# An attention-and-experts kernel: the remainders of the experts in blocks of two halves, and the last stage with rows added three pieces later

## The chip, the cores and the metric

The kernel runs on one NeuronCore of a Trainium2 chip. The core has five engines that run side by side, each through its own list of instructions in order: TensorE (matrix products, in the profile PE, its weight loads PEld), VectorE (DVE), ScalarE (ACT), GpSimd (POOL) and SyncE (SP), which here does nothing but issue transfers. Sixteen DMA engines carry the transfers between main memory (HBM) and the on-chip memory (SBUF). The metric is the device time of one execution in microseconds (us); lower is better.

## The reference

The reference normalises each row of `x` (4 batches of 1024 rows, 512 wide) and adds two things to the row: causal attention with 16 heads of width 32 and a distance penalty (ALiBi), and a mixture of experts.

```python
xn = _layernorm(x, axis=-1)
x = x + _L0_attn_ref(xn, Wq, bq, ..., Wo, bo) + _L0_ffn_ref(xn, gate_w, w1, w2)

# _L0_ffn_ref: 8 experts, each row goes to its best two
logits = jnp.einsum('th,eh->te', x, gate_w)
topw, sel = jax.lax.top_k(_softmax(logits), 2)
topw = topw / jnp.sum(topw, axis=-1, keepdims=True)
gate_up = jnp.einsum('th,eoh->eto', x, w1)      # 512 -> 2 * 352
g, u = jnp.split(gate_up, 2, axis=-1)
expert_out = jnp.einsum('eti,ehi->eth', _silu(g) * u, w2)   # 352 -> 512
out = jnp.einsum('eth,te->th', expert_out, combine)
```

The kernel computes an expert only for the rows that chose it: 4096 rows with two choices are 8192 (row, expert) pairs. All values are float32.

## The kernel before

**Routing.** After the layer norm (rows kept in HBM as `xr_d`, their transposes as `xn_d`), `route` (lines 479 to 594) sorts the pairs by expert on DVE: it counts the pairs of each expert, rounds the count up to whole blocks of 128, and gives each pair a slot (`slot`), each block an expert (`eid`) and each slot a row (`token`). With 8 experts whose counts are not known at build time, rounding up can take 71 blocks (`NBLK`, line 76), so 71 blocks are always computed, whatever share of them is padding. A few projections stand between the pieces of `route` on PE.

**Experts.** `expert_pieces` (lines 675 to 805) makes three pieces a block. `gate(k)` transposes the activation of block k-1 (`pact`) and multiplies the block's rows by the first half of the expert's `w1` (`pgate`: four products of 128 x 352); `up(k)` multiplies by the second half (`pup`), issues the loads of the next block's `w1` (four transfers of 352 KB from SP, line 684) and transposes the next block's rows (`pxs`); `second_layer(k)` multiplies block k-1 by `w2` (`ye`: three products of 512 columns), stores the result in `ys_d` (line 786), issues the next `w2` loads (line 695), and has POOL gather the rows of block k+3. Tiles of `w1` come from a ring of six buffers, those of `w2` from a ring of four. A load waits, on SP, until the last reader of its buffer is done, and everything behind it on SP waits with it.

**Attention.** Sixteen units (4 batches x 4 groups of 4 heads) of 12 groups g each. For a group, PE makes scores (`s`), the products that find each row's maximum for the next unit (`m`), and probabilities times values (`o`); ACT takes exponentials, DVE maxima and sums. The `o` products use 128 x 32 pieces of the array: the four heads are four products side by side in four strips of 32 columns.

**The last stage.** `final_pieces` (lines 812 to 862) finishes rows in 32 pieces of 128: `load(i)` issues from SP the rows of `x` (`xr`, line 819) and, for batches 0 to 2, the attention output (`ot`, line 824), and from POOL two gathers of expert rows (`g`, line 828), one for each choice. `piece(i)` adds the two gathered tiles to `xr` on DVE (line 850), multiplies `ot` by `Wo` on PE (`y`, line 840), adds the product to `xr` on DVE (line 843) and stores `xr` from SP (line 844). Every fourth piece belongs to batch 3, whose attention is still being computed: it has no `ot` and no product here, and its rows are held until `rest`. `final_all` (lines 1117 to 1139) puts the pieces in order and loads three pieces ahead: `load` of piece k+3, then `piece(k)`. `xr` and `ot` have four buffers each, `g` eight.

**Order.** The order on every engine is the order of the program. `fill` (lines 1187 to 1213) spreads the list `fills` (expert pieces, then pieces of the last stage, each with a weight) over the groups of the attention, so that at every group the weights spent keep pace with an even rate. A piece of the experts or of the last stage thus stands in PE's list between attention products, and an engine whose next instruction waits does nothing else meanwhile.

Of the kernel before, what the change touches and what calls it, by code (L numbers as in the profile page):

```python
# [16 lines left out]
P = 128  # L17
# [11 lines left out]
def kernel(  # L29
# [46 lines left out]
    NBLK = (T * TOP - NE) // BLK + NE  # L76
# [6 lines left out]
    eid = const.tile([P, NBLK], U32, tag="eid", name="eid")  # L83
# [29 lines left out]
    with ExitStack() as actx:  # L113
# [287 lines left out]
        def set_route():  # L401
# [13 lines left out]
            steps = ramp("steps", NB, BLK)  # L415
# [63 lines left out]
        def route():  # L479

            def prefix(src, n, name):
# [8 lines left out]

            more = after_norm("more", [P, NE, NB])
# [4 lines left out]
                ALU.is_gt,  # L496
            )
            blocks = once("blocks", [P, NE])
            nc.vector.tensor_reduce(blocks, more, mybir.AxisListType.X, ALU.add)
            ends = prefix(blocks, NE, "ends")  # L500
            first = once("first", [P, NE])
            nc.vector.tensor_tensor(first, ends, blocks, ALU.subtract)
            nc.vector.tensor_scalar(first, first, float(BLK), None, ALU.mult)
            rank = once("rank", [P, NT, NE])
            nc.vector.tensor_tensor(
                rank, p_rank, first.unsqueeze(1).to_broadcast([P, NT, NE]), ALU.add
            )
            slotf = once("slotf", [P, TOP, NT])
            for j in range(TOP):
# [3 lines left out]

            bnum = once("bnum", [P, NBLK])
            over = after_norm("over", [P, NBLK, NE])
            nc.vector.tensor_tensor(
                over,
                iota_row[:, :NBLK].unsqueeze(2).to_broadcast([P, NBLK, NE]),
                ends.unsqueeze(1).to_broadcast([P, NBLK, NE]),
# [3 lines left out]
            nc.vector.tensor_scalar(eid, bnum, float(NE - 1), None, ALU.min)  # L523
# [150 lines left out]

        def expert_pieces():
            es, w1s, w2s, rows, xsT, acts, actT = {}, {}, {}, {}, {}, {}, {}

            def load_w1(k):
                if k == NBLK:
                    return  # L680
                es[k] = nc.sync.value_load(eid[0:1, k : k + 1], min_val=0, max_val=NE - 1)
                for c in range(NC):
                    w = phase["ex"].tile([P, 2, FI], F32, tag="w1", name=f"w1_{k}_{c}", bufs=6)
                    nc.sync.dma_start(
                        w.rearrange("p g f -> p (g f)"),
                        w1r[bass.ds(es[k], 1), :, c, :].rearrange("o p f -> p (o f)"),
                    )
                    w1s[k, c] = w

            def load_w2(k):  # L690
                if k == NBLK:
                    return
                for f, (f0, m) in enumerate(FCH):
                    w = phase["ex"].tile([P, E], F32, tag="w2", name=f"w2_{k}_{f}", bufs=4)
                    nc.sync.dma_start(
                        w[:m, :],
                        w2T[bass.ds(es[k], 1), f0 : f0 + m, :].rearrange("o p e -> p (o e)"),
# [3 lines left out]
            def load_rows(k):  # L701
                if k >= NBLK:
                    return
# [9 lines left out]
            def turn(k):  # L713

                if k == NBLK:
# [7 lines left out]

            def half_up(k, gu):

                ps = bank([P, FI], F32, name=f"p{('gate', 'up')[gu]}_{k}")
                for c in range(NC):
                    nc.tensor.matmul(  # L728
# [8 lines left out]
            def gate(k):  # L737
                turn_act(k - 1)
                if k == NBLK:
                    return  # L740
                ps = half_up(k, 0)

# [5 lines left out]
            def up(k):  # L748
# [4 lines left out]
                load_w1(k + 1)  # L753
                turn(k + 1)

            def turn_act(k):
                if k < 0:
# [12 lines left out]
            def down(k):  # L770
                if k < 0:
                    return
                y = bank([P, E], F32, name=f"ye_{k}")
                a = actT.pop(k)
                for f, (_, m) in enumerate(FCH):
                    nc.tensor.matmul(  # L776
                        y,
                        lhsT=a[:m, f, :],
                        rhs=w2s.pop((k, f))[:m, :],
                        start=(f == 0),  # L780
# [585 lines left out]
```

## Time and profile before

| what | value |
|---|---|
| time, median of 3 runs | 1636.28 us (1635.67 to 1639.81) |
| the profiled execution's own time | 1648.37 us |
| its span, first to last instruction | 1646.6 us |
| PE busy | 1612.0 us, 98% |
| DVE, ACT, POOL busy | 939.4, 890.0, 332.5 us |
| moved by DMA | 278.94 MB, 169 GB/s on average |
| granted TensorE clock, mean | 0.997 of full |

Busy is time in which an instruction of the engine ran; an engine's waiting shows as an idle time in front of an instruction, with what ended it. A product of float32 operands is two MATMUL records on PE, so `pgate ... x568` is 71 blocks x 4 products x 2. SP's rows (SPq) are the issues of transfers, not the transfers themselves. All windows and starts are in us from the span's start.

### The profile page before, as it was taken

Reading aid. Unit: us, or ns where it says so; the run is one execution under the profiler, and the core shown is the slowest. Engines: PE = TensorE matmul, PEld = TensorE weight load, DVE = VectorE, ACT = ScalarE, POOL = GpSimd, SP = SyncE. Lnnn points to the kernel's source line nnn. Section 1 sums busy time; section 2 is a strip of 40 time slices with the busy share of each in tenths; the row PEclk is TensorE's granted clock in tenths of the full one; section 3 lists DMA queues with packets and bytes.
Section 4 is the critical chain, followed back from the end, with each engine's and each line's share of the span. In section 5 each row is a group of like instructions: output and inputs, shape, how many; then the busy total and the mean of one; then the engine's idle time right before and its main releaser. Section 6 shows DMA issues by size and latency. Waiting matters only on the chain.

```text
span 1646.6 us, 29019 instructions
## 1 busy us (share of the span) xinstructions
PE 1612.0 (98%) x9476; PEld 785.9 (48%) x9476; DVE 939.4 (57%) x2886; ACT 890.0 (54%) x2062; POOL 332.5 (20%) x762
## 2 busy tenths in 40 slices
PE   7999999999999999999999999999999999979999
PEld 4545545545454544545544445454444445433333
DVE  6775555655646555555555555555555555547652
ACT  5443455565656465656556474646565565646331
POOL 4610011111020102021111112010211011133660
PEclk9999999999999999999999999999999999999999
DMA  9847854547542434456452335464533424356891
GB/s 312 334 138 255 276 168 155 193 132 237 168 135 89 144 125 146 145 184 209 136 161 88 116 97 174 147 232 153 171 124 105 137 90 156 119 188 200 275 300 64
DMA packets 146486, 278.94 MB, mean 169 GB/s; under 512 B 16448, under 2 KB 45120, under 8 KB 144800
## 3 DMA queue, kind: packets, MB, share of 16 engines
q1 hardware_dynamic: 134384, 234.89, 43.3%
q0 software_dynamic: 10800, 35.40, 7.4%
q10 hardware_dynamic: 1152, 6.82, 1.0%
q8 instruction: 75, 1.23, 0.3%
q14 instruction: 75, 0.61, 0.1%
HBM read 229.07 MB, written 47.97 MB: 168 GB/s over the span
## 4 chain that ended last, share of the span: by engine, by line
PE 88%; DMA 2%; issue 1%; ACT 1%; DVE 1%; SPq 0%; another core or an unknown queue 0%; DVEq 0%; ACTq 0%
PE ye L776 11%; PE pup L728 11%; PE pgate L728 10%; PE s L1007 10%; PE o L1084 8%; PE m L893 8%; PE pk L622 6%; PE pq L622 6%; PE y L840 6%; PE pv L654 5%; PE s L1026 2%; PE pxs L721 2%; PE pact L762 2%; DMA w<-in_w1T 2%; DMA ot<-o_d 1%
## 5 line engine op out<-in xcount | busy, mean ns | idle before, releaser
L1038 ACT ACTIVATE pr<-s,kbias 128x512 f32<-128x512 f32 (+3 forms) x768 | 382.6, 581 | 387.9 <-PE s L1026 345.9
L939 ACT ACTIVATE z<-z,top 128x896 f32<-128x896 f32 (+7 forms) x512 | 391.5, 773 | 84.0 <-DVE top L929 81.0
L1046 POOL TENSOR_SCALAR_AFFINE_SELECT pr<-pr 128x128 f32<-128x128 f32 x512 | 150.4, 302 | 1105.5 <-ACT pr L1038 1099.0
L917 DVE CUSTOM_DVE_ANT_0 z<-m,rel 128x512 f32<-128x512 f32 (+3 forms) x512 | 271.5, 586 | 101.5 <-PE m L893 101.0
L776 PE MATMUL ye<-w,actT 128*128 128x512 f32 (+1 forms) x426 | 197.9, 600 | 2.1 <-DVE actT L765 2.1
L728 PE MATMUL pgate<-w,xsT 128*128 128x352 f32 x568 | 183.9, 464 | 1.8 <-DMA w<-in_w1T 1.4
L728 PE MATMUL pup<-w,xsT 128*128 128x352 f32 x568 | 182.4, 464 | 0.2 <-ACT pr L1038 0.2
L1007 PE MATMUL s<-q,k 32*128 32x512 f32 (+3 forms) x1536 | 179.4, 533 | 0.0
L893 PE MATMUL m<-k,q 32*128 32x512 f32 (+3 forms) x1536 | 172.5, 487 | 4.9 <-DVE oT L1099 4.8
L917 DVE CUSTOM_DVE_ANT_0 z<-m,rel,l 128x128 f32<-128x128 f32 (+3 forms) x256 | 125.8, 547 | 86.6 <-PE m L893 86.1
L1084 PE MATMUL o<-pr,v 128*32 128x512 f32 (+3 forms) x1536 | 144.9, 492 | 0.0
L728 PEld LDWEIGHTS pup<-w,xsT 128*128 128x128 f32 x568 | 105.6, 190 | 68.7 <-ACT pr L1038 9.9
L728 PEld LDWEIGHTS pgate<-w,xsT 128*128 128x128 f32 x568 | 101.5, 190 | 54.3 <-DMA w<-in_w1T 6.2
L622 PE MATMUL pq<-xnT,wq 128*128 128x512 f32 x256 | 119.6, 610 | 1.3 <-ACT pr L1038 0.8
L776 PEld LDWEIGHTS ye<-w,actT 128*128 128x128 f32 (+1 forms) x426 | 76.6, 190 | 90.7 <-issue 72.5
L622 PE MATMUL pk<-xnT,wk 128*128 128x512 f32 x256 | 117.8, 603 | 0.7 <-ACT pr L1038 0.7
L654 PE MATMUL pv<-wv_sb,xnT 128*128 128x512 f32 x256 | 117.0, 600 | 0.2 <-ACT pr L1038 0.2
L1007 PEld LDWEIGHTS s<-q,k 32*128 32x128 f32 x1536 | 61.1, 183 | 108.9 <-issue 82.3
L893 PEld LDWEIGHTS m<-k,q 32*128 32x128 f32 x1536 | 87.2, 185 | 45.5 <-issue 11.7
L745 DVE SCALAR_TENSOR_TENSOR th<-th,pgate 128x352 f32<-128x352 f32 x71 | 37.0, 521 | 121.7 <-ACT th L744 121.7
L939 ACT ACTIVATION_READ_ACCUMULATOR z<-z,top 128x1 f32 x512 | 100.4, 196 | 0.0
L840 PE MATMUL y<-wo_sb,ot 128*128 128x512 f32 x192 | 90.8, 622 | 6.0 <-DMA ot<-o_d 6.0
(165 smaller groups left out, 1564.1 us busy)
## 6 DMA issues: line engine op xcount, KB each, us to landing
w<-in_w1T SPq DMA_DIRECT2D x284, 352.0 KB
w<-in_w2T SPq DMA_DIRECT2D x142, 256.0 KB
ys_d<-yr SPq DMA_DIRECT2D x71, 256.0 KB
w<-in_w2T SPq DMA_DIRECT2D x71, 192.0 KB
xr<-in_x SPq DMA_DIRECT2D x32, 256.0 KB
out<-xr SPq DMA_DIRECT2D x32, 256.0 KB
xn_d<-xT ACTq DMA_DIRECT2D x6, 1024.0 KB
o_d<-oT SPq DMA_DIRECT2D x24, 256.0 KB
```

Source lines behind the costliest of these rows:

```text
L622: nc.tensor.matmul(ps, lhsT=ws[which][:, i, :], rhs=xnT[b, s][:, i, :], start=(i == 0), stop=(i == NC - 1),)
L654: nc.tensor.matmul(ps, lhsT=xnT[b, t // QT][:, i, (t % QT) * P : (t % QT + 1) * P], rhs=wv_sb[:, i, :], start=(i == 0), stop=(i == NC - 1),)
L728: nc.tensor.matmul(ps, lhsT=xsT[k][:, c, :], rhs=w1s[k, c][:, gu, :], start=(c == 0), stop=(c == NC - 1),)
L776: nc.tensor.matmul(y, lhsT=a[:m, f, :], rhs=w2s.pop((k, f))[:m, :], start=(f == 0), stop=(f == NF - 1),)
L840: nc.tensor.matmul(y, lhsT=lhsTs[c], rhs=wo_sb[:, c, :], start=(c == 0), stop=(c == NC - 1))
L893: nc.tensor.matmul(pss[h][:, col : col + n], lhsT=qs[b, c, s][r, (i % QT) * P : (i % QT + 1) * P], rhs=ks[b, c, k0 // QB][r, :n], start=Tr ...
L917: nc.vector.tensor_tensor_reduce(out=zs[h][:, z0 : z0 + n], in0=pss[h][:, col : col + n], in1=rel[:, S - L + k0 : S - L + k0 + n], scale=1 ...
L939: nc.scalar.activation(z[h][:, z0 : z0 + L], z[h][:, z0 : z0 + L], AF.Exp, bias=top[:, h : h + 1], scale=-slopes[c * HC + h], accum_out=to ...
L1007: nc.tensor.matmul(ps[:, :n], lhsT=ks[b, c, j // QT][r, (j % QT) * P : (j % QT + 1) * P], rhs=qs[b, c, s][r, q0:], start=True, stop=False,)
L1038: nc.scalar.activation(pr[:, :n], pss[h][:, :n], AF.Exp, bias=kbias[:, hh, d : d + 1], scale=-slopes[hh],)
L1046: nc.gpsimd.affine_select(out=pr[:, :P], in_=pr[:, :P], compare_op=ALU.is_ge, fill=0.0, base=0, pattern=[[1, P]], channel_multiplier=-1,)
L1084: nc.tensor.matmul(o[h * D : (h + 1) * D, q1:], lhsT=vs[b, j][:, col : col + D], rhs=prs[h][:, : QB - q1], start=(k == 0), stop=(k == len( ...
```

## The change

Three things change together.

**Blocks of two halves.** Only full blocks of an expert stay blocks of one expert: 57 of them (`PURE`, 8192/128 - 7). What is left of each expert (less than 128 pairs) is rounded up to halves of 64, and two halves, of one or of two experts, make a mixed block: 11 of them, in all 68 blocks. A mixed block is spread evenly among the others in the order `blocks`. Its products are made in strips: four products with 32 of the block's columns each, two with the weights of the first half's expert and two with those of the second (`strips`), in `gate`, `up` and `down`. It so needs the weights of two experts: eight `w1` transfers of 352 KB (six at once, the last two after `gate`) and eight for `w2` in two parts of half the columns, out of the same rings of six and four buffers. Where a mixed block is concerned, `down` of the block before moves ahead of `up`, and its own `down` is two parts, one on each side of the next `up`. `route` computes the layout by halves on DVE, with some 27 instructions more.

**First rows of the last stage.** `x` rows and attention output of the first three pieces go into buffers that are left over by then (one of `xnT`, and that of `Wv`); their loads are issued four pieces before the end of the experts, and the first product `y` stands before the last `down`.

**Gathered rows later.** `piece(i)` is now the product `y` and its addition alone. A new `join(i)` adds the two gathered tiles, and then stores; it stands in the step of piece i+3 (sooner at the end). Loads are issued in the step two pieces ahead, after that step's `join`, in place of three pieces ahead; gathers follow the join. The rings keep their sizes (`xr` and `ot` four, `g` eight).

```diff
-    NBLK = (T * TOP - NE) // BLK + NE
+    HALF = BLK // 2
+    PURE = T * TOP // BLK - (NE - 1)
+    NBLK = PURE + (2 * (NE - 1) + NE) // 2
...
+            full = small("full")
+            nc.vector.tensor_reduce(full, more, mybir.AxisListType.X, ALU.add)
...
+            nc.vector.tensor_tensor(rank, p_rank, every_tile(rows_full), ALU.is_ge)
+            nc.vector.tensor_tensor(rank, rank, every_tile(far), ALU.mult)
+            nc.vector.tensor_tensor(rank, rank, every_tile(first), ALU.add)
+            nc.vector.tensor_tensor(rank, rank, p_rank, ALU.add)
...
+            for n in range(NBLK - PURE):
+                blocks.insert((n + 1) * NBLK // (NBLK - PURE) - 3, PURE + n)
...
+                if mixed(k):
+                    load_two(k, 0, 0)
+                    load_two(k, 0, 2)
+                    load_two(k, 1, 0)
+                    return
...
+            def load_two(k, gu, c):
+                for i, e in enumerate(es[k]):
+                    w = w1_tile(f"{k}_{gu}_{c}_{i}")
+                    nc.sync.dma_start(
+                        w,
+                        w1r[bass.ds(e, 1), :, c : c + 2, gu * FI : (gu + 1) * FI].rearrange(
+                            "o p c f -> p (o c) f"
+                        ),
+                    )
...
+            def strips(ps, tokens, ws, **flags):
+                for q in range(P // D):
+                    cols = slice(q * D, (q + 1) * D)
+                    nc.tensor.matmul(
+                        ps[cols, :],
+                        lhsT=tokens[:, cols],
+                        rhs=ws[q * D // HALF],
+                        skip_group_check=True,
+                        **flags,
+                    )
...
             def gate(k):
...
                 ps = half_up(k, 0)
+                if mixed(k):
+                    load_two(k, 1, 2)
...
+                elif mixed(j):
+                    downs = [(1.5, lambda j=j, part=part: down(j, part)) for part in range(2)]
+                else:
+                    downs = [(2.8, lambda j=j: down(j))]
+                if mixed(k) or j is not None and mixed(j):
+                    pieces += downs[:1] + ups + downs[1:]
+                else:
+                    pieces += ups + downs
...
             def piece(i):
+                xr, o = held[i][:2]
+                if o is not None:
+                    project(b * ST + i, xr, [o[:, c, :] for c in range(NC)])
+
+            def join(i):
                 t = b * ST + i
-                xr, o, gs = held[i]
+                xr, o, *gs = held[i]
                 for j in range(TOP):
                     nc.vector.scalar_tensor_tensor(
                         xr, gs[j], share[:, t, j : j + 1], xr, ALU.mult, ALU.add
                     )
                 if o is not None:
-                    project(t, xr, [o[:, c, :] for c in range(NC)])
+                    store(t, xr)
...
             def prime():
-                for ops_, i in order[:ahead]:
-                    ops_[0](i)
+                o = qkv.tile([P, NC, QB], F32, tag="xnT", name="ot_first", bufs=2)
+                xr = wp.tile([P, NC, E], F32, tag="wv", name="xr_first")
+                for n, (op, i) in enumerate(order[:ahead]):
+                    op[0](i, xr[:, n, :], o[:, :, n * P : (n + 1) * P])
...
+            def late(k):
+                back = (len(order) - 1 - k) // 2
+                return min(back, 3)
...
-                def one(k=k, ops_=ops_, i=i):
-                    if k + ahead < len(order):
-                        nxt, ni = order[k + ahead]
+                def one(k=k, op=op, i=i):
+                    join(k - max(late(k), 1))
+                    if ahead <= k + ahead - 1 < len(order):
+                        nxt, ni = order[k + ahead - 1]
                         nxt[0](ni)
-                    ops_[1](i)
+                    gathered(min(k + 2, unjoined[0] + 3))
+                    if k > 0:
+                        op[2](i)
+                    join(k - late(k))
...
-        PROJ, JOIN = 3.6, 1.5
-        fills = [(0.0, begin_experts)] + expert_pieces() + [(0.0, begin_final), (3.0, finals[0])]
-        fills += [(JOIN if k % B == B - 1 else PROJ, f) for k, f in enumerate(finals[1:])]
+        PROJ, JOIN = 3.6, 0.6
+        fills = [(0.0, begin_experts)] + expert_pieces()
+        fills.insert(len(fills) - 4, (0.0, finals[0]))
+        fills.insert(len(fills) - 1, (PROJ, finals[1]))
+        fills += [(0.0, begin_final), (0.0, finals[2]), (0.0, finals[3])]
+        fills += [(JOIN if k % B == B - 2 else PROJ, f) for k, f in enumerate(finals[4:])]
```

## The prediction

> **What bounds the kernel now.** I read the busy times and the chain first, then the windows by stage, then PE's waits in the last stage.
>
> ```profile
> PE 1612.0 (98%) x9476; PEld 785.9 (48%) x9476; DVE 939.4 (57%) x2886; ACT 890.0 (54%) x2062; POOL 332.5 (20%) x762
> PE 88%; DMA 2%; issue 1%; ACT 1%; DVE 1%; SPq 0%; another core or an unknown queue 0%; DVEq 0%; ACTq 0%
> ```
>
> PE is the bound: only work taken off PE, or waits of PE, move the time. The windows tell where it waits (columns: stretch, its length, PE busy, PEld, DVE, ACT, POOL, granted clock, DMA share, GB/s).
>
> ```profile
> 80.00:106.00 26.00, 22.95 (x106) 11.66 (x105) 23.57 (x35) 12.35 (x26) 1.42 (x2) 1.00 0.03 6
> 160.00:1450.00 1290.00, 1286.21 (x7893) 631.04 (x7893) 718.46 (x2253) 749.63 (x1755) 187.77 (x513) 1.00 0.47 152
> 1450.00:1490.00 40.00, 30.77 (x165) 12.91 (x164) 19.71 (x55) 16.03 (x42) 17.46 (x27) 0.91 0.63 204
> 1490.00:1600.00 110.00, 105.59 (x555) 43.71 (x558) 76.46 (x161) 47.43 (x100) 65.37 (x82) 0.98 0.84 267
> ```
>
> In the expert stage PE idles 3.8 of 1290 us. In the routing (80 to 106) DVE is the busy one. The last stage has the rest, with DMA at 0.84. PE's waits from 1450 on:
>
> ```profile
> PE y L840 <- DMA ot<-o_d: 6.0, 4, 2.4
> PE m L893 <- DVE oT L1099: 4.8, 2, 4.0
> PE ye L776 <- DVE actT L765: 2.1, 1, 2.1
> PE pi L1063 <- DVE l L917: 0.6, 1, 0.6
> ```
>
> Together 13.5 us. Two of these waits are followed by slow products; a `y` of eight records takes 3.6 to 3.7 us otherwise:
>
> ```profile
> 1484.26 5.87 PE L840 MATMUL y<-wo_sb,ot 128*128 128x512 f32 x8
> ...
> 1552.09 5.37 PE L840 MATMUL y<-wo_sb,ot 128*128 128x512 f32 x8 [2.37 <-DMA ot<-o_d]
> ```
>
> **Part 1, three blocks fewer.** A block on PE, start to start in the timeline:
>
> ```profile
> 733.36 2.63 PE L728 MATMUL pup<-w,xsT 128*128 128x352 f32 x8
> 735.83 0.60 PE L721 MATMUL pxs<-ident,xs 128*128 128x128 f32 x4
> 736.27 2.74 PE L776 MATMUL ye<-w,actT 128*128 128x512 f32 x6
> 738.94 0.93 PE L1007 MATMUL s<-q,k 32*128 32x384 f32 x8
> ...
> 748.39 0.55 PE L762 MATMUL pact<-ident,act 128*128 128x128 f32 x3
> 748.78 2.53 PE L728 MATMUL pgate<-w,xsT 128*128 128x352 f32 x8
> 751.14 2.53 PE L728 MATMUL pup<-w,xsT 128*128 128x352 f32 x8
> ```
>
> `pup` 2.47, `pxs` 0.44, `ye` 2.67, `pact` 0.39, `pgate` 2.36: 8.33 us. Three blocks: **-25.0 us**. Their DVE and ACT work lies beside PE and gains nothing.
>
> **Part 2, eleven blocks in strips.** No row of before has these; the nearest are the `o` products, four strips of 128*32 side by side. In the chain a run of two strip sets takes 1.85 us (512+512 columns), 1.64 (512+384) or 0.79 (256+128): 1.64 ns a column and 0.17 us a run. A `gate` or `up` is then 4 x 352 x 1.64 ns + 0.17 = 2.48 us (2.36 to 2.47 now), a `down` 2 x (3 x 256 x 1.64 ns + 0.17) = 2.86 (2.67 now): 0.1 + 0.1 + 0.2 = 0.4 a block, **+4.5 us**; from -4, if a long run of strips hides its start (four runs of 0.17 a block less), to 8. The Trainium skill (TensorEngine Tiling (Array Packing), Tiling Modes, Key Properties) speaks against it: changing the tiling mode drains the array, with no price given. Taken as additional, another 0.17 for each of the 44 runs would make 7.5 more, 12 in all; but the `o` runs already change modes on both sides, so the 0.17 holds the drain, and I keep the row.
>
> **Part 3, weights of two experts.** SP issues 9 loads more for each mixed block; at some 0.55 us each that is beside PE. Six of eight `w1` tiles start at once. The tight place is the block after: no `down` stands between the mixed `up` and the next `gate`, and in PE's order six of the eleven gaps are 0.9 to 1.9 us. The last two `w1` tiles of that block wait for the second product of the mixed `up`, 1.2 us before its end; a 352 KB load lands 3.1 (quiet) to 4.2 us (median) after issue, from the trace's semaphores, so at 2.0 to 3.5 after the end of `up`. They are read 1.2 and 1.9 us into `gate`: up to 1 us late, six times. In two of the blocks the loads stand behind the `w2` loads of a `down` just before: 2 us more each. Rows are shorter (1408 and 1024 bytes in place of 2816 and 2048); packets of 512, 2048 and 2816 bytes take 27, 84 and 112 ns, so a mixed block costs 11.7 us of all 16 engines against 5.4, in a cycle of 20. I take **+4 us**, from 0 to 55 (5 a block, if every load is late by that difference).
>
> **Part 4, routing.** DVE runs without a break from 78.6 to 102.6 and PE waits for it at 97.40:
>
> ```profile
> 81.07 0.42 DVE L505 TENSOR_TENSOR rank<-routing,first 128x256 f32<-128x256 f32 x1
> 97.40 1.19 PE L539 MATMUL routing<-both,place 128*128 128x142 bf16 x16 [2.16 <-DVE both L572]
> ```
>
> New: 13 small instructions and a prefix sum of 6 at 0.16 (3.1), three `rank` steps at 0.43 (1.3), a table of 352 elements made and reduced at 0.53 each with three small steps (1.6), less 0.3 for a smaller `over`: 5.7 us, all before the first `place`. PE has no work to cover it: **+5.5 us** (3 to 7).
>
> **Part 5, the last stage.** The waits at its beginning go: `y` of the first three pieces has its rows early, and joins no longer stand in front of it: -13.5, and -5.1 for the slow clock after two waits (below).
>
> What is late next: a buffer of `xr` is now held from its load, two steps before the product, to the store after the join, three steps behind. With four buffers and three of four pieces using them, the load for a product waits for the landing of the store that SP issued just before it. In SP's order it stands directly behind that store, with that store's semaphore. Before, one other store lay between. Queued behind the load on SP: its `ot` load, the next store, the next loads. PE waits for `ot`. At `y8` (counting products from 0) the chain to `y10` is: addition of `y8` 0.85 after its end, two joins at 0.75, issue of the store 0.4, its landing, issue of `xr` 0.5, then `ot`. Landing of a store: 2.05 (the 71 `ys_d` stores, median) to 3.6, the store of 1544.73 here, which released the load of 1548.35:
>
> ```profile
> 1544.73 0.34 SPq L844 DMA_DIRECT2D out<-xr  x1
> ...
> 1546.06 0.52 SPq L824 DMA_DIRECT2D ot<-o_d  x1
> 1546.98 0.34 SPq L844 DMA_DIRECT2D out<-xr  x1
> 1548.35 0.33 SPq L819 DMA_DIRECT2D xr<-in_x  x1
> ```
>
> I take 2.6. Landing of `ot`: 3.7 (the same 256 KB in 512-byte pieces as `wq`, quiet) to 5.9 (the `ot` of 1546.06, for which PE waited at 1552.09); I take 4.5. Sum 10.4 us; 9.0 to 12.6. Beside it lie, in PE's order, only `y9` (3.5) and a group's narrow scores (1.1): 4.6. So `y10` waits **5.8 us** (4.4 to 8). The same place recurs every three products: before `y7` (where the join stands behind four maxima on DVE), `y10`, `y13`, `y16`, `y19`: 5 x 5.8 = 29. Before `y4`, whose load follows the first join, 4; before `y21` 1.5. In all **+34** (25 to 50). The gathers, issued three to four steps ahead of the join, are covered by 15 us and cost nothing; without that cover each join, and so each of these loads, would be late by what is missing.
>
> **The clock.** Windows 1470 to 1490 and 1540 to 1560 were granted 0.83 and 0.91 of the clock: half speed for 6.8 and 3.6 us, after waits of 4.0 and 2.4 us, so 3.4 and 1.8 us lost. The Trainium skill (TensorE: Matmul & The Clock Gate, Part 1) has the array throttle to half after an idle window of about 3.4 us and recover after 3.4 us of work, which is 1.7 lost a time: five waits make 8.5; by the rows' mean of 2.6, **+12.5**. A wait of 2.4 us sufficed here, which is shorter than the page's window; I take the rows.
>
> **Sum.** -25.0 + 4.5 + 4 + 5.5 - 18.6 + 34 + 12.5 = **+17 us**. The profiled execution took 1648.4 us around its span of 1646.6, 12 above the median of the timed runs; the difference is applied to the median: **1653 us**.
>
> **Rivals.**
> 1. Late loads in the last stage, as summed: 1653, with its own ends (parts 2 to 5) 1640 to 1672. Chance 0.55.
> 2. The loads come in time: if store and `ot` land so quickly, or joins run so early, that the 10.4 us fit in the 4.6 beside them, the last stage has neither wait nor slow clock, and -25 + 4.5 + 4 + 5.5 - 18.6 leaves **1607**. Against it: the sum of the quiet ends is still 9.0. It decides where the late loads and the clock cost under 30 of their 46. 0.16.
> 3. Half of it: 2 to 3 us at each place, too short for the clock: +18 in place of 46, 1625 to 1640, about **1636**, no change. 0.14.
> 4. The doubled weights become the bound of the expert stage: 5 us more at each mixed block, the upper end of part 3, gives 1653 + 51 = **1704**. For it: 4.3 MB a mixed block in short rows; against it: DMA at 0.47 in that stage. 0.15.
>
> **How the numbers follow.** A measurement of this kernel tells changes over about 0.3% (4.9 us) from none. Slower: 0.52 from rival 1, 0.15 from 4, 0.03 from 3: 0.70. Same: 0.03 + 0.06: 0.09. Faster: 0.16 + 0.05: 0.21. Range: rival 1's ends, and from there toward 2 down to 1618 and toward 4 up to 1685, so that about 0.1 is left out on each side.
>
> **What will show it.** Part 1 and 2: about 8.3 us of PE for each block kept, strip groups at 0.6 us a set of four. Part 3: PE waits on `w` loads, none to a few us in all. Part 4: a wait of some 6 us in front of the first `routing` products. Part 5: PE waits on `ot` of 4 to 8 us every third product, granted clock near 0.8 there, SP waiting for `out` stores. The prediction is wrong if these waits are absent, or if waits on `w` exceed 10 us.

## The result and the profile after

The changed kernel takes **1723.6 us** (median of four runs, 1716.1 to 1728.2), the kernel before in the same runs 1636.0: a ratio of 1.053 (95% interval 1.049 to 1.057). The prediction had the sign, with 1653, and was 71 us too low. The profiled execution of the changed kernel took 1728.2 us, its span 1726.3, 79.7 more than the span before.

Page of the changed kernel, busy times and chain:

```profile
PE 1630.7 (94%) x10379; PEld 773.9 (45%) x10379; DVE 937.4 (54%) x2909; ACT 887.3 (51%) x2056; POOL 330.2 (19%) x759
PE 87%; DMA 6%; DVE 3%; issue 1%; ACT 1%; SPq 1%; ACTq 0%; DVEq 0%
```

PE is busy 19 us longer with three blocks less, and DMA, 2% of the chain before, is 6% of it. The windows by stage (stretch, length, PE, PEld, DVE, ACT, POOL, granted clock, DMA share, GB/s):

```profile
80.00:112.00 32.00, 26.27 (x110) 13.70 (x109) 28.02 (x64) 12.03 (x26) 2.54 (x3) 0.89 0.05 16
160.00:1510.00 1350.00, 1311.49 (x8893) 627.06 (x8894) 730.68 (x2313) 764.33 (x1796) 189.33 (x522) 0.99 0.50 160
...
1550.00:1700.00 150.00, 117.93 (x540) 46.65 (x538) 71.86 (x128) 39.67 (x84) 68.25 (x94) 0.89 0.63 197
```

In the expert stage PE now idles 38.5 of 1350 us where it idled 3.8 of 1290. In the last stage it idles 32 of 150, and the DMA share there is *lower* than before (0.63 against 0.84). That speaks for transfers that are late, not for too many of them; `e7_three_ahead` below tests it. PE's waits, largest first:

```profile
PE y L1005 <- DMA ot<-o_d: 30.8, 7, 6.8
PE pgate L867 <- DMA w<-in_w1T: 21.6, 9, 9.2
...
PE ye_None L918 <- DMA w<-in_w2T: 6.4, 2, 3.9
PE routing L596 <- ACT both L618: 5.2, 1, 5.2
PE pgate L846 <- DMA w<-in_w1T: 3.5, 3, 2.1
```

To compare kernels I split each span into three parts. *Idle* is the time with no PE instruction running. Of the busy time inside the windows that the record of the granted clock shows at half speed, one half is counted as *lost to the clock*. The rest is *PE work at full speed*. For the expert stage (first `pgate` to last `ye`) and the last stage (from there on) idle and clock are given apart; what is missing from their sum lies in the routing.

| kernel | span | full-speed work | clock, all | idle, all | experts: clock, idle | last stage: clock, idle |
|---|---|---|---|---|---|---|
| before, profile shown | 1646.6 | 1607.1 | 4.9 | 34.6 | 0.0, 7.3 | 4.9, 15.5 |
| before, a second profile | 1637.2 | 1603.1 | 7.7 | 26.3 | 1.7, 7.8 | 4.3, 7.1 |
| changed | 1726.3 | 1596.9 | 33.8 | 95.6 | 16.0, 41.5 | 14.9, 38.6 |
| new blocks only | 1667.2 | 1591.3 | 20.1 | 55.8 | 13.4, 31.6 | 4.1, 9.2 |
| new last stage only | 1674.6 | 1605.9 | 12.5 | 56.2 | 0.0, 5.7 | 12.5, 38.8 |
| changed, six rows | 1716.4 | 1596.9 | 27.5 | 92.1 | 11.8, 46.9 | 13.3, 30.3 |
| changed, six rows, loads three ahead | 1678.8 | 1593.3 | 20.0 | 65.4 | 15.8, 42.7 | 1.6, 8.1 |
| the same, eight weight buffers, loads at the gate | 1657.6 | 1594.7 | 11.0 | 51.9 | 6.6, 28.6 | 1.7, 8.5 |
| the same, second layer behind the up instead | 1635.7 | 1594.9 | 2.4 | 38.4 | 0.0, 15.3 | 0.0, 8.0 |
| 71 blocks, new last stage, loads three ahead | 1628.2 | 1603.1 | 0.0 | 25.1 | 0.0, 5.4 | 0.0, 7.6 |

The saving is there (10 us of PE work), and buried under 61 us of idle time and 29 us of half clock: 50 of these 90 in the expert stage, 33 in the last.

### The profile page after: what moved, and what is told of

Read it like the earlier page. It is cut to its first block, busy times and chain, and to the rows that moved or that the text cites. A ratio compares the mean times of both kernels' runs of the same rounds, so it can differ in the third digit from the quotient of the medians.

```text
span 1726.3 us, 31156 instructions
## 1 busy us (share of the span) xinstructions
PE 1630.7 (94%) x10379; PEld 773.9 (45%) x10379; DVE 937.4 (54%) x2909; ACT 887.3 (51%) x2056; POOL 330.2 (19%) x759
## 4 chain that ended last, share of the span: by engine, by line
PE 87%; DMA 6%; DVE 3%; issue 1%; ACT 1%; SPq 1%; ACTq 0%; DVEq 0%
PE s L1179 9%; PE ye_None L918 9%; PE pgate L867 8%; PE pup L867 8%; PE o L1256 8%; PE m L1065 7%; PE pk L679 7%; PE pq L679 7%; PE y L1005 6%; PE pv L711 6%; DMA w<-in_w1T 3%; PE s L1198 2%; PE ye L846 2%; DMA ot<-o_d 2%; PE pxs L839 2%; PE pact L901 1%
## 5 line engine op out<-in xcount | busy, mean ns | idle before, releaser
L867 PE MATMUL pgate<-w,xsT 128*128 128x352 f32 x456 | 158.1, 487 | 22.3 <-DMA w<-in_w1T 21.6
L1089 DVE CUSTOM_DVE_ANT_0 z<-m,rel,l 128x128 f32<-128x128 f32 (+3 forms) x256 | 125.9, 547 | 92.2 <-PE m L1065 92.1
L918 PE MATMUL ye_None<-w,actT 128*128 128x512 f32 x342 | 162.5, 611 | 7.2 <-DMA w<-in_w2T 6.4
L867 PE MATMUL pup<-w,xsT 128*128 128x352 f32 x456 | 147.0, 465 | 0.8 <-ACT pr L1210 0.8
L867 PEld LDWEIGHTS pgate<-w,xsT 128*128 128x128 f32 x456 | 83.4, 197 | 72.2 <-DMA w<-in_w1T 17.4
L867 PEld LDWEIGHTS pup<-w,xsT 128*128 128x128 f32 x456 | 84.2, 190 | 55.5 <-ACT pr L1210 8.2
L918 PEld LDWEIGHTS ye_None<-w,actT 128*128 128x128 f32 x342 | 62.3, 193 | 85.7 <-issue 67.8
```

The costliest lines, as they stand in the source:

```text
L867: nc.tensor.matmul(ps, lhsT=xsT[k][:, c, :], rhs=w1s[k, c][:, gu, :], start=(c == 0), stop=(c == NC - 1),)
L918: nc.tensor.matmul(y, lhsT=a[:m, f, :], rhs=w2s.pop((k, f))[:m, :], **flags)
L1089: nc.vector.tensor_tensor_reduce(out=zs[h][:, z0 : z0 + n], in0=pss[h][:, col : col + n], in1=rel[:, S - L + k0 : S - L + k0 + n], scale=1 ...
```

## The experiments

### Which half of the change costs

`e1_blocks_only` is the changed kernel with the last stage of before; `e2_last_only` is the kernel before with its 71 blocks and the new last stage.

> The new blocks, with the last stage of before. Theory (both parts cost, each in its own stage): the trace after lost 33 us in the last stage against before, so without that the kernel takes 1724 - 33 = 1690 us, with PE waits on w of some 30 us and half clock behind them. Rival (the last stage is what costs, and the blocks about pay for themselves, as the prediction had it): 1620 to 1640 us.

> The 71 blocks and the routing of before, with the new last stage. Theory (both parts cost separately): 1636 + 33 = 1669 us, with waits on ot of some 30 us and half clock. Rival (the last stage is late only because the mixed blocks' transfers run into it): 1617 to 1640 us, waits on ot under 8 us.

Measured: **1669.4** (ratio 1.020, 1.018 to 1.022) and **1677.7** (1.025, 1.023 to 1.027). Each half loses, by 32 and 40 us, together 72 of the 88. PE's waits in the first, then in the second:

```profile
PE pgate L867 <- DMA w<-in_w1T: 21.9, 12, 6.0
```

```profile
PE y L850 <- DMA ot<-o_d: 33.8, 8, 6.6
```

These are the waits of the changed kernel, each with its own half. They are two separate faults. The blocks alone neither lost as much as I expected nor gained. The 15 us that the halves leave lie mostly in the expert stage, where idle and clock make 45.0 in `e1_blocks_only` and 57.5 in the changed kernel. The mixed blocks stand between other attention products in the two kernels, because the weights of the last stage's pieces also set the rate of `fill`; that this is the reason was not tested.

### The last stage: which wait in the chain

The prediction made the held `xr` buffer, and so the landing of a store, the cause. `e3_six_rows` gives the rows six buffers in place of four (and takes two from the gathered rows), so no load has to wait for the store just before it.

```diff
-                        bufs=4 if b < B - 1 else ST,
+                        bufs=6 if b < B - 1 else ST,
...
-                    g = phase["fin"].tile([P, E], F32, tag="g", name=f"g{t}_{j}", bufs=8)
+                    g = phase["fin"].tile([P, E], F32, tag="g", name=f"g{t}_{j}", bufs=6)
...
-                    gathered(min(k + 2, unjoined[0] + 3))
+                    gathered(min(k + 2, unjoined[0] + 2))
```

> The changed kernel with six xr buffers in place of four, and six gather buffers in place of eight to make room (gathers then run one piece less ahead). Theory (the loads wait for the landing of the store just before them, since a row buffer is held five steps): waits on ot fall from 31 us to under 8, half clock in the last stage goes, 1724 - 40 = 1684 us. Rival (the loads are late because SP issues them behind the join, or because DMA is full): waits on ot stay above 20 us, 1710 to 1724 us.

Measured: **1720.2** (ratio 1.052, 1.049 to 1.054), waits on `ot`:

```profile
PE y L1005 <- DMA ot<-o_d: 25.3, 7, 4.7
```

Only about 1 us at each place went. The expectation was wrong, and not even the prediction's own sum supports it: without the landing of 2.6, its chain of 10.4 is still 7.8 against 4.6 beside it. One of these places in e3:

```profile
1617.44 0.34 SPq L1011 DMA_DIRECT2D out<-xr  x1
1617.84 0.42 SPq L982 DMA_DIRECT2D xr<-in_x  x1
...
1618.35 0.52 SPq L987 DMA_DIRECT2D ot<-o_d  x1
...
1624.12 2.79 PE L1005 MATMUL y<-wo_sb,ot 128*128 128x512 f32 x3 [4.57 <-DMA ot<-o_d]
```

The load now leaves 0.4 us after the store, with no landing between; in the changed kernel it leaves 2 to 4 us after it at six of the seven places. But `ot` then takes longer: the product that waits for it starts 5.8 us after its issue in the median of the seven places, against 5.0, which gives back part of the gain. What still keeps the load is that it stands *behind* the join's store in SP's list, whatever buffer it goes to. The timeline of the changed kernel shows the whole chain at the longest wait:

```profile
1594.55 3.70 PE L1005 MATMUL y<-wo_sb,ot 128*128 128x512 f32 x8
...
1598.29 0.69 DVE L1008 TENSOR_TENSOR xr<-y,xr 128x512 f32<-128x512 f32 x1 [3.00 <-PE y L1005]
...
1599.26 3.70 PE L1005 MATMUL y<-wo_sb,ot 128*128 128x512 f32 x8
...
1599.49 2.98 DVE L1022 SCALAR_TENSOR_TENSOR xr<-g,share,xr 128x512 f32<-128x512 f32 x4
...
1601.06 0.35 SPq L1011 DMA_DIRECT2D out<-xr  x1
...
1604.91 0.33 SPq L982 DMA_DIRECT2D xr<-in_x  x1
...
1605.34 0.53 SPq L987 DMA_DIRECT2D ot<-o_d  x1
...
1609.94 2.90 PE L1005 MATMUL y<-wo_sb,ot 128*128 128x512 f32 x3 [6.76 <-DMA ot<-o_d]
```

The product ends at 1598.25. Addition, another DVE operation and the first join bring the store to 1601.06; its landing takes 3.85; `ot` is there 4.6 after its issue. That is 11.7 us, and beside it PE has one product. (The last row counts only the records inside the view.) Loads are now issued two steps ahead, behind a join that is behind the addition of the last product; before, three ahead.

`e7_three_ahead` is the same with the third step given back, `e5_join_one_later` the changed kernel with the join one piece late in place of three.

On e3, for e7:

```diff
-                    if ahead <= k + ahead - 1 < len(order):
-                        nxt, ni = order[k + ahead - 1]
+                    if k + ahead < len(order):
+                        nxt, ni = order[k + ahead]
```

On the changed kernel, for e5:

```diff
-                return min(back, 3)
+                return min(back, 1)
```

> The changed kernel with six buffers for the rows and six for the gathered rows, as in the run before, and in addition the loads of a piece issued three steps ahead again in place of two; joins stay three pieces late. The theory now: SP takes its queue in order, so the rows of piece k+2 are issued only behind the store of the join that DVE does after the addition of piece k-1; addition 0.85, join 1.5, store 0.4, issue 1.2, landing 4 to 6 us make 8 to 10 us, and two products with their scores cover about 5. One step more is another 3.6 us and more, so the waits on o rows fall from 25 us to under 8, the half clock in the last stage from seven windows to at most two, and the time to 1680 to 1695 us. Rival: the DMA engines are full (busy share 0.69 to 0.84 in that stage) and the landing grows with what is asked for; then 15 to 30 us of waits stay and the time is 1710 to 1725.

> The changed kernel with the gathered rows added one piece later in place of three, everything else the same (four buffers for rows, loads two steps ahead). Theory of the queue: the load of piece k+2 stands behind the join and the store on SP as before, only that its buffer is free earlier; waits on o rows 20 to 35 us, time 1708 to 1726. Rival, that of the prediction (the buffer is held too long by the late join): the buffer is free two steps earlier, no load waits for a landing, waits on o rows under 8 us, time 1675 to 1690.

Measured: e7 **1681.2** (ratio 1.029, 1.026 to 1.031), e5 **1715.8** (1.048, 1.046 to 1.050). Waits of e7, then of e5:

```profile
PE y L1005 <- DMA ot<-o_d: 3.0, 3, 2.5
```

```profile
PE y L1005 <- DMA ot<-o_d: 20.4, 10, 4.1
...
PE y L1005 <- issue: 6.6, 1, 6.6
```

One step more of distance removes 22 us of waits and, by the table, 12 us of half clock in the last stage: 39 us between e3 and e7. The same bytes are moved, so full DMA engines, the rival, are not the cause. A join that comes earlier leaves the chain as it is, since the load stays behind it: waits on `ot` fall by 10 us, and a new one of 6.6 stands beside them. So the distance in SP's list is the cause. The six buffers are its condition: with three steps ahead and joins three steps late, six pieces are held at once, up to five of them in the ring of `xr`, so four buffers could not have had that distance.

With that repaired, what is the new last stage worth? `e9_last_three` is e2 (71 blocks) with the edits of e3 and e7; `e14_three_late1` is e9 with joins one piece late.

> The 71 blocks of before with the new last stage, and in it six buffers for rows, six for gathered rows and loads three steps ahead: the last stage of the change without its late loads. Theory (the late loads and the slow clock after them are all that the new last stage costs; what is left is the prediction's saving of up to 18.6 us): 1615 to 1632 us, waits on o rows under 5 us. Rival (the later joins and the additions left at the end cost something of their own): 1634 to 1650 us with no wait on o rows.

> The 71 blocks of before and the new last stage with loads three steps ahead (1632.5 us), with the gathered rows added one piece later in place of three. Theory (once loads are in time the lateness of the join is free on either side; the queue decides): within 3 us, 1629.5 to 1635.5. Rival (joins three pieces late are what keeps PE fed): 1637 to 1645 us.

Measured: e9 **1632.5** against 1636.6 beside it (ratio 0.9983, 0.9970 to 0.9996), so the late loads and the clock behind them made up 45 us of e2's time. e14 ran on a chip on which the kernel before takes 1646.1, so only its ratio compares: 1.000 (0.998 to 1.002). Waits of e9 on `ot`, then those of e14, which has a second kind that e9's profile has not:

```profile
PE y L850 <- DMA ot<-o_d: 2.6, 4, 0.9
```

```profile
PE y L850 <- DMA ot<-o_d: 6.1, 4, 2.0
PE y L850 <- issue: 5.2, 4, 4.3
```

The intervals of the two overlap; whether the two further pieces of lateness give anything is not settled. e9 is the best kernel of this study, by an amount below what I said a measurement can tell.

### The expert stage: bytes, buffers, or the place in the queue

`e4_one_expert` loads, for a mixed block, only the weights of the first half's expert and uses them for both halves: a mixed block then loads as many bytes as any other, still in the short rows. The edit of `load_two` is shown; the two loops of `load_w2` are changed in the same way.

```diff
-                for i, e in enumerate(es[k]):
+                for i, e in enumerate(es[k][:1]):
...
-                        w1s[k, gu, c + d, i] = w[:, d, :]
+                        w1s[k, gu, c + d, 0] = w1s[k, gu, c + d, 1] = w[:, d, :]
```

> The changed kernel, but a mixed block loads the weights of its first half's expert alone and uses them for both halves (it leaves out the second expert: half the weight traffic of mixed blocks, the products unchanged). Theory (the doubled loads are late): waits on w fall from 31 us to under 8 and half clock goes with them, 1724 - 50 = 1674 us. Rival (strips, or the moved down, cost the time on PE): 1710 to 1724 us.

Measured: **1704.0** (ratio 1.041, 1.040 to 1.043), between the two: the loads saved bring 20 us, and the longest wait is still 6.9 us (9.2 in the changed kernel).

```profile
PE pgate L867 <- DMA w<-in_w1T: 14.1, 9, 6.9
PE ye_None L918 <- DMA w<-in_w2T: 9.7, 5, 3.3
```

The other remedies were one buffer size and one order: `e8_eight_w1` has eight `w1` buffers, so that all eight tiles of a mixed block fit; `e6_down_after_up` puts the second layer back behind the mixed `up`. For the room, e8 takes one of three buffers from the gathered tokens (`xs`) and one of two from the results (`ye`).

```diff
-            ahead_of = dict(zip(blocks, blocks[3:]))
+            ahead_of = dict(zip(blocks, blocks[2:]))
...
-                return phase["ex"].tile([P, 2, FI], F32, tag="w1", name=f"w1_{name}", bufs=6)
+                return phase["ex"].tile([P, 2, FI], F32, tag="w1", name=f"w1_{name}", bufs=8)
...
                     load_two(k, 1, 0)
+                    load_two(k, 1, 2)
...
                 ps = half_up(k, 0)
-                if mixed(k):
-                    load_two(k, 1, 2)
```

For e6:

```diff
-                if mixed(k) or j is not None and mixed(j):
+                if j is not None and mixed(j):
                     pieces += downs[:1] + ups + downs[1:]
```

> The changed kernel with eight buffers for first-layer weights in place of six (gathered tokens two buffers in place of three and fetched two blocks ahead, the result row one buffer in place of two), so that all eight tiles of a mixed block can be loaded during the block before, and none of the block after it waits for a product of the mixed one. Theory (the last tiles of the block after a mixed one are late, and the second tiles of the mixed one itself, for want of buffers): waits on first-layer weights fall from 25 us to under 10, time 1690 to 1705. Rival (twice the bytes in short rows are the limit, or the order on SP): waits stay above 18 us, time 1712 to 1728.

> The changed kernel with the second layer of the block before a mixed one put back behind the mixed block's up product, where it lies between that and the next gate again. Theory (too few buffers, whatever the order): the tiles that the mixed up takes are then asked for 1.2 us before its first use and come 2 to 3 us late, those of the next block are in time: the waits move and their sum stays within 8 us of 25, time 1712 to 1732. Rival (the missing second layer before the next gate is the whole of it): waits on first-layer weights under 10 us, time 1690 to 1705.

Measured: e8 **1739.4** (ratio 1.063, 1.061 to 1.065), e6 **1712.0** (1.047, 1.044 to 1.050). Waits of e8, then of e6:

```profile
PE pgate L868 <- DMA w<-in_w1T: 20.9, 10, 9.4
PE pxs L840 <- DMA xs<-xr_d,token: 11.9, 5, 4.5
```

```profile
PE pup L846 <- DMA w<-in_w1T: 16.5, 12, 5.4
```

Buffers alone leave the waits on `w1` where they were (20.9 at the next `gate`, 21.6 in the changed kernel). That e8 is 16 us slower, outside both expectations, goes with a new wait of 11.9 on the gathered tokens, of which it has two buffers in place of three. The order alone moves the wait from the next `gate` to the mixed `up`, as expected. The timeline of the changed kernel around its longest wait:

```profile
750.26 2.57 PE L846 MATMUL pgate<-w,xsT 128*32 128x352 f32 x32
...
756.36 0.34 SPq L930 DMA_DIRECT2D ys_d<-yr  x1
...
756.90 1.00 SPq L794 DMA_DIRECT2D w<-in_w2T  x2
...
758.16 0.91 SPq L805 DMA_DIRECT2D w<-in_w2T  x2
...
758.56 2.57 PE L846 MATMUL pup<-w,xsT 128*32 128x352 f32 x32
...
759.11 0.90 SPq L656 DMA_DIRECT2D xnT<-xn_d  x2
...
761.62 2.59 SPq L768 DMA_DIRECT2D w<-in_w1T  x4
...
771.63 4.74 PE L867 MATMUL pgate<-w,xsT 128*128 128x352 f32 x8 [9.19 <-DMA w<-in_w1T]
```

The four `w1` loads of the next block are issued behind four `w2` loads and, here, behind 2 MB of `xnT`. They come out when the mixed `up` has ended, and only two short groups stand between it and the `gate` that reads them; the first lands 9.9 us after its issue, where the loads of the other mixed blocks take 3 to 7. With eight buffers (e8) the four loads leave at the same place, behind the same transfers and 0.2 us after the end of the mixed `up`:

```profile
766.49 2.97 SPq L769 DMA_DIRECT2D w<-in_w1T  x4
```

In the changed kernel four `w2` loads stand ahead of these loads in all eleven mixed blocks. In four of the eleven all four `w1` loads come out after the end of the mixed `up`, by 0.5 to 4.9 us. In one of these other work covers it; the other three make 16.7 of the 21.6 us of waits.

`e10_at_gate` takes e7 and e8 and issues these four loads behind the mixed `gate`, ahead of the `w2` loads; `e11_after_up8` takes e7, e8 and e6 in place of that. Both gather tokens at the start of a block, against the new wait of e8. The edits of e10 in `gate` and `up`:

```diff
                 ps = half_up(k, 0)
+                if mixed(k):
+                    load_w1(follow.get(k))
...
-                load_w1(follow.get(k))
+                if not mixed(k):
+                    load_w1(follow.get(k))
```

> The kernel with loads three steps ahead (1681 us) and eight first-layer buffers; in it the four loads for the block after a mixed one are issued behind the mixed gate, ahead of the second-layer loads in SP's queue, in place of behind its up; tokens are gathered at the start of a block in place of at its end. Theory (the place in SP's queue: these loads stand behind four second-layer loads, and in one case behind 2 MB for the next projections, and are issued one product before they are read): waits on first-layer weights fall from 25 us to under 8, half clock from 52 us to under 30, time 1645 to 1662. Rival (the bytes themselves: a mixed block moves 4.3 MB in short rows): waits stay over 15 us, time over 1672.

> The same with the other remedy: the loads stay behind the mixed up, but the second layer of the block before stands between that up and the next gate again, as it does in all other blocks, and eight buffers let all the mixed block's own tiles come one block earlier. Theory: as for the run before, 1645 to 1662 and waits on first-layer weights under 8 us. Rival (bytes): over 1672.

Measured: e10 **1659.0** (ratio 1.013, 1.011 to 1.015), e11 **1644.6** (1.004, 1.003 to 1.006), from 1681.2 of e7. In e10 the same place reads:

```profile
743.51 2.57 PE L847 MATMUL pgate<-w,xsT 128*32 128x352 f32 x32
...
744.93 2.09 SPq L769 DMA_DIRECT2D w<-in_w1T  x4
...
750.14 1.01 SPq L795 DMA_DIRECT2D w<-in_w2T  x2
...
751.81 2.57 PE L847 MATMUL pup<-w,xsT 128*32 128x352 f32 x32
...
755.75 2.63 PE L868 MATMUL pgate<-w,xsT 128*128 128x352 f32 x8
```

The loads are issued 1.4 us behind the start of the mixed `gate` in place of 11.4, and 11 us before they are read. The wait is gone, with the same bytes, and PE's order between `up` and the next `gate` is the same in both kernels at all eleven mixed blocks. Waits on `w1` fall from 25.3 in e7 to 4.4 in e10 and 3.7 in e11; those on `w2`, 8.1 in e7, stay in e10 (8.5) and halve in e11. The lines of e7, e10 and e11:

```profile
PE pgate L867 <- DMA w<-in_w1T: 23.0, 11, 9.5
```

```profile
PE pgate L847 <- DMA w<-in_w1T: 2.6, 5, 1.6
...
PE pgate L868 <- DMA w<-in_w1T: 1.8, 3, 0.8
```

```profile
PE ye L847 <- DMA w<-in_w2T: 3.6, 6, 1.2
...
PE pgate L868 <- DMA w<-in_w1T: 1.9, 2, 1.5
```

So the place in the queue decides, once there are buffers to load into: eight alone (e8) or the order alone (e6) left over 20 us of waits. The loads at the gate with six buffers weren't tried. The bytes come second: with fewer of them (e4) the longest wait is shorter and stays.

### The missing PE work, and the profile of before

The rows say that three blocks fewer save 25 us and strips cost 4; the table shows 6 to 16 us less work. `e13_no_strips` is e11 with one product of full width in place of four strips. It takes the weights of the two experts in turn and so leaves out the split by halves; the lines that choose the weights are not shown. `e15_after_up8_again` is e11 beside it, on the chip of e14.

```diff
-                for q in range(P // D):
-                    cols = slice(q * D, (q + 1) * D)
-                    nc.tensor.matmul(
-                        ps[cols, :],
-                        lhsT=tokens[:, cols],
-                        rhs=ws[q * D // HALF],
-                        skip_group_check=True,
-                        **flags,
-                    )
+                nc.tensor.matmul(ps, lhsT=tokens, rhs=ws, **flags)
```

> The kernel with eight weight buffers, the second layer behind the mixed up and loads three steps ahead (1644.6 us), with the strips of the eleven mixed blocks made one product of full width each: all weights of both experts are loaded as before, but a mixed block's rows are multiplied with a mixture of the two experts' weights, so that its sums are not the reference's. Theory (a strip block costs 0.3 us more than a whole one, as its rows show): PE's busy time at full speed 1589 to 1593 in place of 1594.9, time 1637 to 1644. Rival (the strips cost the 12 us of PE time that are missing from the three blocks, in the instructions beside them): 1578 to 1584, time 1626 to 1634.

> The same kernel with its strips, once more beside the run without them: 1640 to 1648 us if its first profile (span 1635.7) was at the lower end of its spread, 1636 to 1639 if that profile was the rule.

Measured: e13 **1641.5** (ratio to before 0.9965, 0.9948 to 0.9982), e15 **1649.4** (1.0005, 0.9991 to 1.002). Without strips the time is 7.9 us less. The full-speed work is 9.1 less than in e15 (1596.8 to 1587.6) and 7.3 less than in e11: 0.7 to 0.8 us for each mixed block, where the strips' own rows show 0.3 (from start to start, 2.39 to 2.50 for a `gate`, 2.50 for an `up`, 2 x 1.44 for a second layer, against 2.46, 2.42 and 2.67 of a whole block). That is neither expectation for the work. The rest lies in small amounts in other groups, among them `pxs`, `pq`, `pact` and `plg`, and I can't say by what way, or how much of it is spread between runs: the work of two profiles of the same kernel differs by 2 to 4. Nor do strips explain all that is missing: even without them the work is only 15.5 to 19.5 us under that of the two profiles of before, where three blocks make 25. These 5 to 10 us stay open. In the end the repaired blocks save nothing: e11 is 0.4% slower than the kernel before, and e15, the same kernel, equal to it.

> The kernel before once more, for a second profile: the first one took 1648 us, 12 over the median of its timed runs. If that was one disturbed stage, this profile has a span of 1632 to 1638 with the difference in PE's idle time at one place; if all profiles of it are so long, 1645 to 1648.

Measured: 1639.0 us, span 1637.2. The first profile of before had been unlucky in one stage, the last. In the second its waits are:

```profile
PE ye L776 <- DVE actT L765: 2.1, 1, 2.1
PE y L840 <- DMA ot<-o_d: 1.7, 1, 1.7
...
PE m L893 <- DVE oT L1099: 0.8, 1, 0.8
```

With the 0.6 of `pi` as before 5.2 us, not 13.5. Of the waits that the change was to remove, the larger part was absent here: it belonged to that one execution.

## Why the prediction was right and wrong

- **Part 1, -25.0.** Right by its rows: a pure block takes 8.43 us in the mean, 8.33 in the sum. The work that PE does in all fell by less, as said above.
- **Part 2, +4.5 (to 8).** The products' lengths were right within 0.1 us each; the whole is 7 to 9 by e13, at the upper end of the range.
- **Part 3, +4 (0 to 55).** This is the step that failed: the lead of the weight loads. It took only the last two `w1` loads for the block behind a mixed one as late, issued 1.2 us *before* the end of the mixed `up` and up to 1 us late, with 2 us more in two blocks for the `w2` loads ahead. Four of the eleven blocks look like that in the trace. In four others all four loads come out *after* the end, behind `w2` loads that the moved second layer put ahead of them, once with 2 MB of `xnT` too. Idle time in the expert stage rose by 34.2 us, and the waits on `w` are 31.5, over the 10 that the prediction named as a sign of being wrong. Rival 4 named the place, priced at 51, with a chance of 0.15, and argued against it with the mean DMA share of 0.47, which says nothing of a load's lead. (By its own figures its 5 a block should be 11.7 - 5.4 = 6.3, so 69 in all in place of 55.)
- **Part 4, +5.5.** The size was right, in part by luck: the first `pgate` stands 6.1 us later, 3.7 by idle time and 2.8 by a half clock that the sum had not priced there. The wait itself grew from 2.2 to 5.2.
- **Part 5, -18.6 and +34.** The size was right: idle in the last stage rose by 23.1, against 34 - 13.5 = 20.5. The chain was right link by link (11.7 at its longest, 10.4 predicted). What it named as the cause, the held buffer and the landing, is 2.6 of the 10.4, and taking it away (e3) brought 0.8 us a place; e3, e5 and e7 show the distance in SP's list. The -18.6 was read from the unlucky profile: e9 gains 3 to 4.
- **The clock, +12.5.** For the last stage about right (14.9 in place of 4.9). What it lacked follows from Part 3: 16.0 more in the expert stage, which the sum had at nothing.
- **The sum.** The changed profile is 79.7 us over the first of before, the sum said 17. The 63 between are: waits of the expert stage 30.2, its clock 16.0, PE work 10.3, the rest 6.2. Rival 4 stood on top of the late loads of the last stage already (1653 + 51 = 1704), and so 20 us under the time measured. That is closer than its parts deserve: it took 21 us too much for the waits and had nothing for the clock of the expert stage and the missing PE work. At its chance of 0.15 the range stopped at 1685. Slips in the sums (five times 2.6 is 13.0; the lower end of Part 2 is -3; Rival 3's +18 makes 1625, not 1636) did not matter.

## What to carry to other kernels

A load's lead is counted in its queue, not in its buffers: write down what stands ahead of it in the issuing engine's list and what that waits for, since a free buffer behind a blocked store is worth little (e3, e8) and a moved piece of compute also moves the loads that it issues. Price several late loads as a sum, and each wait of 2.5 us or more with its slow clock, 1.4 to 3.3 us here where it came. A gain that consists of waits should be read from two profiles of the same kernel before it is counted.

## What the runs showed of the hardware

The half clock is set off by shorter waits than I had thought, and in a graded way. In all 17 traces of this case together, from 60 us on, for PE waits with no other wait over 0.5 us within 8 us (from start to start of the instructions that waited) and no half-speed window already running:

| wait of PE | brings a half-speed window | its length |
|---|---|---|
| 0.8 to 1.0 us | 0 of 27 | |
| 1.0 to 1.5 us | 5 of 35 | 3.4 |
| 1.5 to 2.5 us | 21 of 48 | 3.4, rarely more |
| 2.5 to 3.0 us | 10 of 11 | 3.4 or 6.8 |
| 3.0 to 5.0 us | 35 of 35 | 3.4 or 6.8 |
| over 5.0 us | 34 of 34 | 6.8 (25), 10.2 (8), 3.4 (1) |

The reason for the grades shows in the starts: in every trace all half-speed windows start on one grid of 3.41 us. What counts is how long PE idles within one step of this grid. All steps from 60 us on that ran at full speed:

| idle time of PE in the step | steps | next step at half speed |
|---|---|---|
| under 1.0 us | 4414 | 3 |
| 1.0 to 1.7 us | 108 | 12 |
| 1.7 to 2.0 us | 33 | 20 |
| over 2.0 us | 93 | 93 |

A wait of 2 us thus brings half speed when it falls into one step, and not when it is shared by two. The Trainium skill (TensorE: Matmul & The Clock Gate, Part 1) has an idle window of about 3.4 us; here over 2.0 us within a step of 3.41 were always enough. A window that starts while PE still waits is in part spent waiting: after the 69 waits of 3 us and more the half clock took 1.4 to 3.2 us of time. So a load that is 5 us late costs these 5 us and some 2 to 3 more, and waits under 1 us that stand alone cost nothing more (0 of 27 from 0.8 to 1.0 us).
